# Softmax reciprocals in three bfloat16 parts, and bfloat16 router counts, in an attention and mixture-of-experts kernel

## The chip, the core and the metric

The kernel runs on one core of one Trainium2 chip. The time is the device time of one launch in microseconds (us); lower is better. The core's engines are named as in the profile: PE (TensorE, matrix products), PEld (its weight loads), DVE (VectorE), ACT (ScalarE), POOL (GpSimd) and SP (SyncE, which here only issues DMAs).

## The reference

One transformer layer over x of shape (8, 1024, 256), 16 heads of 16 channels, everything in float32. Cut to what matters here:

```python
scores = einsum('bhid,bhjd->bhij', q, k) * scale + gated_bias   # bias by relative position, gated per query
attn = softmax(scores, axis=-1)
out = einsum('bhij,bhjd->bhid', attn, v)                         # then @ Wo.T + bo
x = layernorm(x + attention(x))

probs = softmax(x_flat @ Wr.T)                                   # router, 8 experts, top 2
for e in range(8):
    elig = (topk_experts == e).any(-1) & ~fallback
    pos = cumsum(elig) - 1                                       # place of each token in expert e
    kept, overflow = elig & (pos < cap), elig & (pos >= cap)     # cap = 2560
    # y of expert e to the kept tokens; the overflow goes to a fallback FFN
x = layernorm(x + moe(x))
```

## The kernel before

The kernel has two stages: attention with the router (until about 2560 us of the profile) and the experts' FFNs (the rest). The change touches the first stage alone.

**Units and steps.** Attention is worked in 64 units: 8 batches times 8 pairs of heads (`HP = 2`). A unit has 16 steps, one for each block of 128 keys (`j`, 8 of them) and each half of the queries (`c`, 512 columns). The loop `for g in range(G + 12)` runs over 1024 steps, `u, s = divmod(g, 16)`. The order of all instructions is written out by hand (`tc.manual_schedule()`), so each engine executes in the order in which the Python code issues.

In a step, `max_fold` (DVE, L1066) first finishes a row maximum; then `streams.held()` reads what a helper task has in its bank; `scores` (PE, L1109) makes two 512-column products; `max_first` and `max_second` (PE, L1025 and L1029) compute exact maxima of the scores 21 steps ahead, in two halves, from bfloat16 parts; `exps` adds the gated bias to the scores (DVE, L1124) and exponentiates (ACT, L1131). On every second step (`c == 1`) `products` (PE, L1139) accumulates probabilities times values in `o_acc`. The values carry a column of ones, so that row `D` of each head's 32 rows of `o_acc` holds the softmax sums. POOL makes the gated biases (`gb`, L985, one for every two steps) and small diagonals (`dgb`, L998).

**Dividing by the sums.** At step 1 of unit `u`, `take_outputs(u - 1)` copies `o_acc` to `osb` (ACT, L1151). The sums lie in 4 rows of 512. Four DMAs move them to 128 partitions x 16, DVE inverts them there (L1172), and four DMAs move them back to 4 rows; `after(n, f)` runs `f` at the n-th following `tick()`, which is in `streams.free()` of each step. So the sums are moved at step 2, inverted at step 4 and moved back at step 5. At step 10 `divide` makes one matmul of `sel` (4 x 128) with the 4 rows (L1179), which spreads the reciprocals over the 16 channels of each head in the one shared PSUM bank (`ps_x`, one buffer); DVE multiplies them onto `osb` (L1183) and four DMAs store the result. All these DMAs are issued by SP, in order, with the loads for unit `u + 2` (`load_unit`, at steps 3, 4 and 6, L907 and L915) and the gates (`load_gates`, L965).

**Helper tasks.** The projections of the next batch (`prologue`), and the output projection, layernorm and router of the batch before (`epilogue`), are Python generators that are advanced once a step, between the steps' own work. A task that needs PSUM takes the shared bank at one step and reads it at the next.

**Counting.** For each expert, POOL makes running counts over the 8 blocks of 128 tokens (`running`, on `prefix` and `incl`, L751), and PE adds them over the partitions (`count`): a product of `ones` with the running counts and one of `later` with `who`, both 128 x 128 by 128 x 8 in float32 (L821, L822). DVE takes the places from it (`place`, `spill`, L835 and L838), and POOL needs `spill` for the next expert. There are 9 such counts for each batch, the last batch's after the loop, where nothing else runs.

**Experts.** Each of 8 experts computes chunks of 512 rows (L1481, L1496), which PE fills.

Of the kernel before, what the change touches and what calls it, by code (L numbers as in the profile page):

```python
# [11 lines left out]
F32 = mybir.dt.float32  # L12
BF16 = mybir.dt.bfloat16
# [3 lines left out]
ALU = mybir.AluOpType  # L17
# [4 lines left out]
P = 128  # L22
H, D = 16, 16
NG, HG = 4, 4
E = H * D
NE, TOP_K = 8, 2
FF = 1024
NBUCKET, MAX_DIST = 80, 200
CH = 512
# [49 lines left out]
def tile_attention_moe(  # L79
# [25 lines left out]
    nc = tc.nc  # L105
    B, N, _ = x.shape
    T = B * N
    NI = N // P
# [44 lines left out]
    with ExitStack() as at:  # L153
        cst = at.enter_context(tc.tile_pool(name="cst", bufs=1))
# [3 lines left out]
        rt = at.enter_context(tc.tile_pool(name="rt", bufs=1))  # L158
# [24 lines left out]
        def load_piece(b, n, tag="xp", bufs=3):  # L183
# [18 lines left out]
            out=gb_ld.rearrange("p g o -> p (g o)"), in_=gru_b.to_broadcast([P, 8])  # L202
# [9 lines left out]
        for sb, src in ((wk_sb, wk), (wq_sb, wq)):  # L212
            for k in range(NK):
                nc.scalar.dma_start(
                    out=sb[:, k, :].rearrange("p (h d) -> p h d", d=D),
                    in_=src[k * P : (k + 1) * P, :].rearrange("p (h w) -> p h w", w=32)[
                        :, :, :D
                    ],
# [3 lines left out]
            out=heads_b[0], in_=kcl[8, :].rearrange("(h w) -> h w", w=32)[:, :D]  # L222
        )
        for g in range(H // HG):
            nc.scalar.dma_start(
                out=heads_b[1, g * HG : (g + 1) * HG, :],
                in_=bq[:, g].rearrange("(r w) -> r w", w=32)[:HG, :D],
            )
        for sb, which in ((bk_sb, 0), (bq_sb, 1)):
            nc.scalar.dma_start(  # L230
                out=sb,
                in_=heads_b[which].rearrange("h d -> (h d)").rearrange("(k p) -> p k", p=P),
# [33 lines left out]
        for base, sign in ((0, 1), (D - 1, -1)):  # L266
            nc.gpsimd.affine_select(
                out=wg, in_=wg, compare_op=ALU.is_ge, fill=0.0, base=base,
                pattern=[[sign * P, NK], [-sign * D, H], [0, 2]], channel_multiplier=sign,
# [6 lines left out]
            out=anti, in_=anti, compare_op=ALU.not_equal, fill=1.0, base=-(P - 1),  # L276
            pattern=[[1, P]], channel_multiplier=1,
        )
        ones = cst.tile([P, P], F32, name="ones")
        nc.gpsimd.memset(ones, 1.0)  # L280
        later = cst.tile([P, P], F32, name="later")
        nc.gpsimd.memset(later, -1.0)
        nc.gpsimd.affine_select(
            out=later, in_=later, compare_op=ALU.is_gt, fill=0.0, base=0,
            pattern=[[-1, P]], channel_multiplier=1,
        )
        sel = cst.tile([4, 4, 32], F32, name="sel")
        nc.gpsimd.memset(sel, 0.0)
        nc.gpsimd.affine_select(
            out=sel, in_=sel, compare_op=ALU.not_equal, fill=1.0, base=0,  # L290
            pattern=[[-1, 4], [0, 32]], channel_multiplier=1,
        )
        rank = cst.tile([P, NE], F32, name="rank")
        nc.gpsimd.iota(
            rank, pattern=[[-1, NE]], base=NE, channel_multiplier=0,
# [4 lines left out]
            number, pattern=[[P, NI]], base=0, channel_multiplier=1,  # L300
# [22 lines left out]
        for lo, hi in zip(cuts[:-1], cuts[1:]):  # L323
# [9 lines left out]
            out=blocks,  # L333
            in_=bass.AP(
                sd.tensor, sd.offset + EDGE + 1 - REACH, [[STRIP, H], [-1, P], [1, WIN]]
            ),
# [15 lines left out]
        for side, bk in enumerate((int(farn[0]), int(far[0]))):  # L352
            nc.sync.dma_start(
                out=farb[:, side, :], in_=rel[bk : bk + 1, :].to_broadcast([P, H])
# [13 lines left out]
        for t in fd:  # L368
# [4 lines left out]
                out=flat, in_=zero16.unsqueeze(1).to_broadcast([P, flat.shape[1], 2 * E])  # L373
# [4 lines left out]
        pattern = once.tile([R_ALL, HP, N], F32, tag="oD", name="pattern")  # L378
        for h in range(HP):
            for part in range(3):  # L380
                r = R_FAR + part * NI
                nc.sync.dma_start(out=pattern[r : r + NI, h, :], in_=kcr[:NI, :])
            for r in range(R_SHIFT, R_ALL):
                nc.sync.dma_start(out=pattern[r : r + 1, h, :], in_=kcr[8:9, :])
        incl = [cst.tile([P, NE + 1, NI], F32, name=f"incl{i}") for i in range(2)]
        prefix = [cst.tile([P, 2 * NI], F32, name=f"prefix{i}") for i in range(3)]
        for t in prefix:
            nc.vector.memset(t, 0.0)
        o_acc = ps_o.tile([P, CH], F32, name="o_acc")
# [54 lines left out]
        def after(n, what):  # L444

            waiting.append([n, what])
# [230 lines left out]
        def epilogue(b, me):  # L677
            xt, oD = me.xt, me.oD
            for t in range(0, NI, 2):
# [3 lines left out]
                for tt in range(2):  # L683
                    for k in range(NK):
# [4 lines left out]
                            start=(k == 0),  # L689
                            stop=(k == NK - 1),  # L690
# [30 lines left out]
            for t in range(0, NI, 2):  # L721
# [13 lines left out]
                for tt in range(2):  # L735
                    for k in range(NK):
                        nc.tensor.matmul(
                            pl[:, tt, :], x1T[:, tt, k, :], wr_sb[:, k, :],
                            start=(k == 0), stop=(k == NK - 1),
# [4 lines left out]
            def small(tag, *shape):  # L744
                return rt.tile([P, *shape], F32, tag=tag, name=f"{tag}{b}")

            def over_e(a):
# [3 lines left out]
                lambda out, a, b, op=op: nc.gpsimd.tensor_tensor(out, a, b, op)  # L751
# [17 lines left out]
            for k in range(TOP_K):  # L769

                m = small(f"top{k}", NI)
                o = small(f"oh{k}", NI, NE)
                first = small(f"first{k}", NI)
# [31 lines left out]
            now, before = incl[b % 2], incl[(b + 1) % 2]  # L805
            live = slice(NI, 2 * NI)
            who = prefix[0][:, live]
# [10 lines left out]

            def count(e):
                pc = bank("pc")[:, :NI]  # L820
                nc.tensor.matmul(pc, ones, now[:, e, :], start=True, stop=False)  # L821
                nc.tensor.matmul(pc, later, who, start=False, stop=True)  # L822
                return pc

            spill = small("spill", NI)
            for e in range(NE):
# [6 lines left out]
                pc = count(e)  # L833
# [13 lines left out]
            sub(fell, ones[:, :NI], stay)  # L847
            yield BANK
            pc = count(NE)
            yield SLOW  # L850
            nc.vector.tensor_scalar(fbrow, pc, float(FB0 - 1), None, ALU.add)
            if b == B - 1:
                yield BANK
                pf = bank("pf")[:, : NE + 1]
                nc.tensor.matmul(pf, ones, now[:, :, NI - 1], start=True, stop=True)
                yield SLOW
                nc.vector.tensor_copy(counts, pf)
            ts = slice(b * NI, (b + 1) * NI)
# [289 lines left out]
        def take_outputs(u):  # L1148
            me = units[u]
            me.osb = work.tile([P, CH], F32, tag="osb", name=f"osb{u}", bufs=1)  # L1150
            nc.scalar.copy(me.osb, o_acc)  # L1151

            def move_sums():
                me.sums = rt.tile([P, 4 * CH // P], F32, tag="sums", name=f"sums{u}")
                for r in range(4):
                    nc.sync.dma_start(
                        out=me.sums[r * 32 : (r + 1) * 32, :],
                        in_=me.osb[r * 32 + D : r * 32 + D + 1, :].rearrange(
                            "o (p n) -> o p n", p=32
                        ),  # L1160
                    )

            def move_back():
                me.recs = rt.tile([4, CH], F32, tag="recs", name=f"recs{u}")
                for r in range(4):
                    nc.sync.dma_start(
                        out=me.recs[r : r + 1, :].rearrange("o (p n) -> o p n", p=32),
                        in_=me.sums[r * 32 : (r + 1) * 32, :],
                    )

            after(1, move_sums)
            after(3, lambda: nc.vector.reciprocal(me.sums, me.sums))  # L1172
            after(4, move_back)

        def divide(u):
            b, hp = divmod(u, UB)
# [139 lines left out]
        for g in range(G + 12):  # L1316
            u, s = divmod(g, STEPS)
# [3 lines left out]
            if g < G:  # L1321
                if sb == 14:
                    assert not streams.of or streams.of[0][0].__name__ == "scatters"
                    if b:
                        streams.start(epilogue(b - 1, batches[b - 1]))
                    streams.start(begin(b))
                if sb == 60:
                    streams.start(rows(b))
                if u + 2 < UNITS:
                    for which, at_ in enumerate((3, 4, 6)):  # L1330
                        if s == at_:
                            load_unit(u + 2, which)
                    if s == 1:
                        load_max_bias(u + 2)
                    if s == 7:
                        clear_max_bias(u + 2)
                if u + 1 < UNITS:
                    if s == 0:
                        load_bias(u + 1)
                    for which, at_ in enumerate((8, 15)):  # L1340
                        if s == at_:
                            load_gates(u + 1, which)
                if m <= G:
                    max_fold(m - 1)
# [18 lines left out]
            others = s + 1 != SHIFT_AT  # L1363
# [10 lines left out]
            if u and s == 1:  # L1374
                take_outputs(u - 1)
            next(clear, None)

        banks += [(ps_m, "pm0"), (ps_m, "pm1")]
        streams.start(epilogue(B - 1, batches[B - 1]))
        streams.drain()  # L1380

# [3 lines left out]
    with ExitStack() as ex:  # L1385
# [11 lines left out]
            place1, pattern=[[P, IPC]], base=1, channel_multiplier=1,  # L1397
# [245 lines left out]
```

## Time and profile before

| | |
|---|---|
| median of 3 runs | 3657.59 us (3646.69 to 3658.37) |
| profiled execution | 3654.03 us, its span 3652.2 us |
| mean granted TensorE clock | 0.963 |
| busy: PE, PEld | 3277.1 us (90%), 1655.8 us (45%) |
| busy: DVE, ACT, POOL | 1935.0 us (53%), 2047.8 us (56%), 2221.9 us (61%) |
| first to last `osb` copy (64 units) | 172.0 to 2471.8 us |
| after the last unit, router of the last batch | about 2490 to 2556 us |

A group line of the profile reads: line, engine, operation, out<-in by the program's names, sizes, count | busy us, mean ns of one | idle time of the engine just before them, and what ended it. A timeline line reads: start us, length us, engine, line, operation; in brackets the idle time before it and what ended that. Busy times of PE include the modelled end of each matmul, so matmuls that follow each other closely show overlapping lengths, and the cost of one is read from the next one's start.

### The profile page before, as it was taken

To read this page: it belongs to the slowest core of one execution; us is meant where nothing else is said; L and a number is where in the kernel's file an instruction comes from. 1 tells how busy PE (TensorE), PEld (TensorE's weight loads), DVE (VectorE), ACT (ScalarE), POOL (GpSimd) and SP (SyncE) were. 2 spreads that over 40 slices of the span, in tenths; PEclk is the share of its full clock that TensorE was granted. 3 is DMA by queue.
4 is the path that set the end of the run, shared out by engine and by line. 5 is a ranking of instruction groups with operands and counts; after the bars stand their busy time and mean duration, and the time that the engine had idled before them with its cause. 6 is when DMAs were issued, how large, how long until landed. Compare 5 with 4: busy or idle time off the path is not lost. (4 is left out here: it accounts for less than half of the span.)

```text
span 3652.2 us, 53430 instructions
## 1 busy us (share of the span) xinstructions
PE 3277.1 (90%) x16263; PEld 1655.8 (45%) x16263; DVE 1935.0 (53%) x5559; ACT 2047.8 (56%) x3084; POOL 2221.9 (61%) x2619
## 2 busy tenths in 40 slices
PE   4798998989999999999999999994399999999997
PEld 2342343334334334334334433333267677667776
DVE  2455656655765665665666576661134344444443
ACT  1577777767777777777787777771022222222222
POOL 2667666876886887787787788782233333333332
PEclk8899999999999999999999999995699999999999
DMA  5567657655643453444444444420332332232220
GB/s 139 159 167 196 190 167 192 186 177 177 186 146 111 139 155 114 130 141 135 125 135 137 133 135 129 132 92 10 113 88 58 88 90 67 85 96 88 72 90 21
DMA packets 380418, 455.71 MB, mean 125 GB/s; under 512 B 87478, under 2 KB 285235, under 8 KB 380107
## 3 DMA queue, kind: packets, MB, share of 16 engines
q1 hardware_dynamic: 338602, 388.06, 35.9%
q0 software_dynamic: 19296, 43.38, 4.2%
q10 hardware_dynamic: 22208, 20.58, 1.9%
q8 instruction: 138, 2.26, 0.3%
q14 instruction: 174, 1.42, 0.1%
HBM read 315.16 MB, written 140.54 MB: 125 GB/s over the span
## 5 line engine op out<-in xcount | busy, mean ns | idle before, releaser
L1131 ACT ACTIVATE pr<-sc 128x1024 f32<-128x1024 f32 x1024 | 1049.0, 1025 | 321.5 <-DVE sc L1124 298.9
L985 POOL TENSOR_TENSOR gb<-bias,gates 128x1024 f32<-128x1024 f32 (+2 forms) x512 | 1070.2, 2091 | 133.6 <-DMA gates<-gd 67.3
L1066 DVE CUSTOM_DVE_ANT_0 over<-pm,over 128x512 f32<-128x512 f32 x1024 | 703.8, 687 | 794.4 <-ACT over L1054 303.9
L1054 ACT ACTIVATE over<-pm 128x512 f32<-128x512 f32 x1024 | 612.7, 598 | 260.9 <-PE pm L1029 242.1
L1109 PE MATMUL sc<-qs,ks 122*128 122x512 bf16 x2048 | 617.4, 382 | 39.2 <-ACT pr L1131 24.7
L1124 DVE TENSOR_TENSOR sc<-sc,gb 128x640 f32<-128x640 f32 (+3 forms) x768 | 599.6, 781 | 77.6 <-POOL gb L985 56.0
L1029 PE MATMUL pm<-biasb,dgb 128*128 128x320 bf16 (+2 forms) x2048 | 579.2, 283 | 0.0
L1139 PE MATMUL o_acc<-pr,v 128*17 128x512 f32 x4096 | 551.9, 610 | 0.3 <-ACT pr L1131 0.3
L1481 PE MATMUL ph<-xsT,w 128*128 128x512 f32 (+1 forms) x1440 | 488.8, 497 | 13.3 <-ACT xsT L1421 12.7
L1496 PE MATMUL py<-w,hT 128*128 128x256 f32 x2208 | 485.0, 379 | 5.5 <-DVE ys L1503 5.5
L1496 PEld LDWEIGHTS py<-w,hT 128*128 128x128 f32 x2208 | 419.2, 190 | 74.1 <-issue 10.5
L1025 PE MATMUL pm<-ks,qs 120*128 120x512 bf16 x1024 | 396.5, 387 | 44.8 <-DVE mh L1066 25.7
L1025 PEld LDWEIGHTS <-qs 120*128 120x128 bf16 x2048 | 207.3, 101 | 505.2 <-issue 339.6
L1025 PE MATMUL pm<-ks_d,qs 120*128 120x512 bf16 x1024 | 393.9, 385 | 39.3 <-DMA qs<-qd 18.0
L1488 ACT ACTIVATE hT<-ph,b_sb 128x512 f32<-128x512 f32 (+1 forms) x360 | 212.3, 590 | 287.9 <-PE ph L1481 264.1
L1481 PEld LDWEIGHTS ph<-xsT,w 128*128 128x128 f32 x1440 | 270.7, 190 | 213.8 <-issue 169.1
L1421 ACT COPY xsT<-pt 128x512 f32<-128x512 f32 (+1 forms) x90 | 39.6, 490 | 567.5 <-PE pt L1418 567.5
L143 POOL TENSOR_TENSOR rs<-rstd,neghalf 128x1 f32<-128x1 f32 x138 | 78.3, 568 | 446.8 <-DVE rstd L141 446.4
L1029 PEld LDWEIGHTS <-dgb 128*128 128x128 bf16 x2048 | 201.7, 98 | 262.5 <-issue 147.2
L998 POOL TENSOR_TENSOR dgb<-anti,grev 128x256 bf16<-128x256 f32 x512 | 313.8, 613 | 4.9
L1109 PEld LDWEIGHTS <-ks 122*128 122x128 bf16 x2048 | 197.5, 99 | 221.4 <-issue 70.4
L419 POOL TENSOR_TENSOR parts<-rest,parts 128x512 bf16<-128x512 f32 (+1 forms) x80 | 92.5, 1157 | 239.7 <-ACT parts L418 193.4
(184 smaller groups left out, 2913.3 us busy)
## 6 DMA issues: line engine op xcount, KB each, us to landing
gates<-gd SPq DMA_DIRECT2D x128, 704.0 KB
biasb<-stripb SPq DMA_DIRECT2D x128, 288.0 KB
bias<-blocks SPq DMA_DIRECT2D x64, 512.0 KB
xd<-zero SPq DMA_DIRECT2D x51, 522.0 KB
ks<-kd SPq DMA_DIRECT2D x384, 64.0 KB
qs<-qd SPq DMA_DIRECT2D x384, 64.0 KB
yd<-zero SPq DMA_DIRECT2D x40, 512.0 KB
w<-in_w_dram ACTq DMA_DIRECT2D x16, 1024.0 KB
```

The source lines that it names most:

```text
L985: nc.gpsimd.tensor_tensor(gb_[:, :, off : off + hi - lo], me.bias[:, :, off : off + hi - lo], gates[:, :, lo - at : hi - at], ALU.mult,)
L998: nc.gpsimd.tensor_tensor(dg, anti.unsqueeze(1).to_broadcast([P, HP, P]), batches[b].grev[:, i, hp * HP : (hp + 1) * HP] .unsqueeze(2) .to ...
L1025: nc.tensor.matmul(pm, QS[u % 3][:R_SHIFT, h, i * P : (i + 1) * P], keys, start=True, stop=False)
L1029: nc.tensor.matmul(pm[:, lo:hi, :], dgb[m - h][:, h, :], me.biasb[:, at : at + (hi - lo) * P].rearrange("p (j n) -> p j n", n=P)[:, :, :HALF],
L1054: nc.scalar.activation(me.over, pm, AF.Relu)
L1066: nc.vector.tensor_tensor_reduce(out=me.over, in0=me.rest, in1=me.over, scale=1.0, scalar=-3.0e38, op0=ALU.add, op1=ALU.max, accum_out=me. ...
L1109: nc.tensor.matmul(me.sc[:, h, :], ks[:, h, j * P : (j + 1) * P], qs[:, h, c * CH : (c + 1) * CH], start=True, stop=True,)
L1124: nc.vector.tensor_tensor(sc[:, :, lo - c * CH : hi - c * CH], sc[:, :, lo - c * CH : hi - c * CH], me.gb[j][:, :, off : off + hi - lo], A ...
L1131: nc.scalar.activation(pr, sc, AF.Exp)
L1139: nc.tensor.matmul(o_acc[r : r + D + 1, :], batches[b].v[:, j, hp * HP + h, :], prs[c][:, h, :], start=(j == 0), stop=(j == NI - 1),)
L1481: nc.tensor.matmul(ph[:, :size], w1_sb[:, k, f * P : (f + 1) * P], xsT[:, k, :size], start=(k == 0), stop=(k == NK - 1),)
L1496: nc.tensor.matmul(py, hT[:, f, t * P : (t + 1) * P], w2_sb[:, f, :], start=(f == 0), stop=(f == NF - 1),)
```

## The change

The reciprocals are made and spread differently, and the counts have other types.

- `sums` is one tile of 128 partitions x 64 for the whole stage, its first 32 partitions filled with 1.0 once. Three DMAs, each of all four rows of sums, write three copies of them to partitions 32 to 127, 64 elements in each partition.
- `first`, at step 4, inverts the whole tile (float32, 128 x 64) and copies it to bfloat16 (`rp`). `others`, at step 5, subtracts the copy from the reciprocals on partitions 64 to 127, copies the rest to bfloat16 there, and subtracts again on partitions 96 to 127. So the three copies become three bfloat16 parts that add up to the reciprocal.
- One DMA, at step 6, moves the 96 partitions back to 12 rows of 512 (`recs`, bfloat16), and the spreading matmul of step 10 has 12 rows and bfloat16 operands; `sel` has its ones in three rows for each head.
- `ones16`, `later16`, `incl` and `prefix` are bfloat16, so the counting matmuls are (the counts stay whole numbers of at most 64 before the sum over partitions).

```diff
-        sel = cst.tile([4, 4, 32], F32, name="sel")
+        sums = cst.tile([P, 4 * CH // 32], F32, name="sums")
+        nc.vector.memset(sums[:32], 1.0)
+        ones16 = cst.tile([P, P], BF16, name="ones16")
+        nc.gpsimd.tensor_copy(ones16, ones)
+        later16 = cst.tile([P, P], BF16, name="later16")
+        nc.gpsimd.tensor_copy(later16, later)
+        sel = cst.tile([12, 4, 32], BF16, name="sel")
...
-        incl = [cst.tile([P, NE + 1, NI], F32, name=f"incl{i}") for i in range(2)]
-        prefix = [cst.tile([P, 2 * NI], F32, name=f"prefix{i}") for i in range(3)]
+        incl = [cst.tile([P, NE + 1, NI], BF16, name=f"incl{i}") for i in range(2)]
+        prefix = [cst.tile([P, 2 * NI], BF16, name=f"prefix{i}") for i in range(3)]
...
-                nc.tensor.matmul(pc, ones, now[:, e, :], start=True, stop=False)
-                nc.tensor.matmul(pc, later, who, start=False, stop=True)
+                nc.tensor.matmul(pc, ones16, now[:, e, :], start=True, stop=False)
+                nc.tensor.matmul(pc, later16, who, start=False, stop=True)
...
             def move_sums():
-                me.sums = rt.tile([P, 4 * CH // P], F32, tag="sums", name=f"sums{u}")
-                for r in range(4):
+                for a in range(3):
                     nc.sync.dma_start(
-                        out=me.sums[r * 32 : (r + 1) * 32, :],
-                        in_=me.osb[r * 32 + D : r * 32 + D + 1, :].rearrange(
-                            "o (p n) -> o p n", p=32
-                        ),
+                        out=sums[(a + 1) * 32 : (a + 2) * 32, :],
+                        in_=me.osb[D::32, :].rearrange("r (p n) -> r p n", p=8),
                     )
+            def first():
+                nc.vector.reciprocal(sums, sums)
+                me.rp = rt.tile([P, 4 * CH // 32], BF16, tag="rp", name=f"rp{u}")
+                nc.vector.tensor_copy(me.rp, sums)
+            def others():
+                nc.vector.tensor_tensor(sums[64:], sums[64:], me.rp[64:], ALU.subtract)
+                nc.vector.tensor_copy(me.rp[64:], sums[64:])
+                nc.vector.tensor_tensor(me.rp[96:], sums[96:], me.rp[96:], ALU.subtract)
             def move_back():
-                me.recs = rt.tile([4, CH], F32, tag="recs", name=f"recs{u}")
-                for r in range(4):
-                    nc.sync.dma_start(
-                        out=me.recs[r : r + 1, :].rearrange("o (p n) -> o p n", p=32),
-                        in_=me.sums[r * 32 : (r + 1) * 32, :],
-                    )
+                me.recs = rt.tile([12, CH], BF16, tag="recs", name=f"recs{u}")
+                nc.sync.dma_start(
+                    out=me.recs.rearrange("q (p n) -> q p n", p=8), in_=me.rp[32:]
+                )
             after(1, move_sums)
-            after(3, lambda: nc.vector.reciprocal(me.sums, me.sums))
-            after(4, move_back)
+            after(3, first)
+            after(4, others)
+            after(5, move_back)
```

In the built program PE, ACT and POOL keep their order otherwise. SP's order changes in one place: the move back stands behind the seven loads of step 6 (`qs<-fd`, `qs<-qd`) and no longer in front of them.

More of the change, by code (lines that the diff above doesn't have):

```diff
@@ L286, in tile_attention_moe @@
         )
-        sel = cst.tile([4, 4, 32], F32, name="sel")
-        nc.gpsimd.memset(sel, 0.0)
-        nc.gpsimd.affine_select(
-            out=sel, in_=sel, compare_op=ALU.not_equal, fill=1.0, base=0,
-            pattern=[[-1, 4], [0, 32]], channel_multiplier=1,
-        )
+        sums = cst.tile([P, 4 * CH // 32], F32, name="sums")
[5 more added lines that the diff above has]
+        sel = cst.tile([12, 4, 32], BF16, name="sel")
+        nc.gpsimd.memset(sel, 0.0)
+        for a in range(3):
+            nc.gpsimd.affine_select(
+                out=sel, in_=sel, compare_op=ALU.not_equal, fill=1.0, base=-4 * a,
+                pattern=[[-1, 4], [0, 32]], channel_multiplier=1,
+            )
         rank = cst.tile([P, NE], F32, name="rank")
@@ L384, in tile_attention_moe @@
                 nc.sync.dma_start(out=pattern[r : r + 1, h, :], in_=kcr[8:9, :])
-        incl = [cst.tile([P, NE + 1, NI], F32, name=f"incl{i}") for i in range(2)]
-        prefix = [cst.tile([P, 2 * NI], F32, name=f"prefix{i}") for i in range(3)]
+        assert B * NI <= 256
+        incl = [cst.tile([P, NE + 1, NI], BF16, name=f"incl{i}") for i in range(2)]
+        prefix = [cst.tile([P, 2 * NI], BF16, name=f"prefix{i}") for i in range(3)]
         for t in prefix:
@@ L854, in epilogue @@
                 pf = bank("pf")[:, : NE + 1]
-                nc.tensor.matmul(pf, ones, now[:, :, NI - 1], start=True, stop=True)
+                nc.tensor.matmul(pf, ones16, now[:, :, NI - 1], start=True, stop=True)
                 yield SLOW
@@ L1153, in move_sums @@
             def move_sums():
-                me.sums = rt.tile([P, 4 * CH // P], F32, tag="sums", name=f"sums{u}")
-                for r in range(4):
+                for a in range(3):
                     nc.sync.dma_start(
-                        out=me.sums[r * 32 : (r + 1) * 32, :],
-                        in_=me.osb[r * 32 + D : r * 32 + D + 1, :].rearrange(
-                            "o (p n) -> o p n", p=32
-                        ),
-                    )
-            def move_back():
-                me.recs = rt.tile([4, CH], F32, tag="recs", name=f"recs{u}")
-                for r in range(4):
-                    nc.sync.dma_start(
-                        out=me.recs[r : r + 1, :].rearrange("o (p n) -> o p n", p=32),
-                        in_=me.sums[r * 32 : (r + 1) * 32, :],
-                    )
+                        out=sums[(a + 1) * 32 : (a + 2) * 32, :],
+                        in_=me.osb[D::32, :].rearrange("r (p n) -> r p n", p=8),
+                    )
+            def first():
[6 more added lines that the diff above has]
+                nc.vector.tensor_tensor(me.rp[96:], sums[96:], me.rp[96:], ALU.subtract)
+            def move_back():
+                me.recs = rt.tile([12, CH], BF16, tag="recs", name=f"recs{u}")
+                nc.sync.dma_start(
+                    out=me.recs.rearrange("q (p n) -> q p n", p=8), in_=me.rp[32:]
+                )
             after(1, move_sums)
-            after(3, lambda: nc.vector.reciprocal(me.sums, me.sums))
-            after(4, move_back)
+            after(3, first)
+            after(4, others)
+            after(5, move_back)
         def divide(u):
```

## The prediction

> **What bounds it.** I read the page's shares and slices first: PE, with the highest share, is busy in nine tenths and more of nearly every slice, and the granted clock is 0.96 to 1.00 in the attention stage once it runs.
>
> ```profile
> PE 3277.1 (90%) x16263; PEld 1655.8 (45%) x16263; DVE 1935.0 (53%) x5559; ACT 2047.8 (56%) x3084; POOL 2221.9 (61%) x2619
> ...
> PE   4798998989999999999999999994399999999997
> ```
>
> Then I cut the stage into its 64 units by the score matmuls. The mean is 36.7 us. Units 8k+5 and 8k+6 take 31 us with PE idle for 0.4 to 0.7. Two steps without helper work take 1.15 + 2.2 = 3.35 us, and the starts of PE's own matmuls account for 3.3: PE sets the pace. In units 8k+7 and 8k POOL also issues 16 scatters (1.01 us each), and the score adds start as POOL's `gb` ends; there POOL sets it, and PE time saved is worth nothing.
>
> By groups (busy, mean ns):
>
> ```profile
> L1179 PE MATMUL pb<-recs,sel 4*128 4x512 f32 x128 | 72.5, 646 | 19.0 <-DMA recs<-sums 9.0 <-DVE dif L651 5.2 <-DVE mh L1066 2.8
> ...
> L1172 DVE RECIPROCAL sums<-sums 128x16 f32<-128x16 f32 x64 | 15.7, 245 | 15.8 <-DMA sums<-osb 15.1 <-issue 0.6
> ```
>
> Every float32 matmul runs as two passes (x128 for 64 units), and so do the counts (L821 and L822, 144 passes each). PE's timeline around one spreading matmul:
>
> ```profile
> 1908.90 1.12 PE L1179 MATMUL pb<-recs,sel 4*128 4x512 f32 x2
> 1909.96 0.39 PE L1025 MATMUL pm<-ks,qs 120*128 120x512 bf16 x1
> 1910.18 0.25 PE L1029 MATMUL pm<-biasb,dgb 128*128 128x192 bf16 x1
> 1910.27 0.59 PE L1109 MATMUL sc<-qs,ks 122*128 122x512 bf16 x2
> 1912.44 0.38 PE L1025 MATMUL pm<-ks_d,qs 120*128 120x512 bf16 x1 [1.57 <-DMA qs<-qd]
> ```
>
> **Spreading matmul.** Start to next start is 1.06 us. A bfloat16 matmul of 512 columns takes 0.22 from start to next start (1909.96 to 1910.18); with part of a weight load (98 ns in L1029's row) I take 0.26. Gain 0.80 in the 48 units that POOL does not pace: 38 us. Bounds: 24 (0.5 each, if DVE's reads in steps 10 to 12, 3.9 us, end last) and 54 (0.85 in all 64).
>
> **Counts.** In the loop a count's four passes hold PE for 0.36 to 0.46 us before the next matmul. Two bfloat16 products with hidden loads should take 0.16 (between 0.06 and 0.2, two loads of L1029's row). That is 0.25 x 63 = 16 us, of which I count 70%, since some fall in steps where PE waits: 11 (bounds 0 and 20). The last batch's nine counts are a bare chain: POOL's `incl` ends at 2530.52, DVE's `place` starts at 2531.63, 1.11 us later. Half the passes save half: 0.55 x 9 + 0.4 for the last sum = 5 (3 to 7). POOL's 128x8 operations take 198 ns, fixed cost at that size; I leave them, and so the five setup operations on POOL, which run beside the first loads (1.5 us if they did not).
>
> **SP's queue.** SP issues `sums` (four, 2.44 us), the loads of steps 3 and 4, and then, without a pause:
>
> ```profile
> 1904.69 2.44 SPq L1166 DMA_DIRECT2D recs<-sums  x4
> 1907.18 0.55 SPq L907 DMA_DIRECT2D qs<-fd  x1
> 1907.77 2.67 SPq L915 DMA_DIRECT2D qs<-qd  x6
> ```
>
> One of four 0.61-us issues goes, and 2.44 us no longer stand in front of `qs<-qd`, so those loads land 3.05 us earlier. PE waits for them at step 11 in 13 units (18 us in all, as in the 1.57 above); all these waits are shorter than 3.05. About half lie in units that POOL paces: gain 9 (0 to 18). The move back itself is now behind the seven loads, so its last issue ends 2.45 us before `qs<-qd` ended, and small DMAs land 1.4 to 1.8 us after that (the sums issued until 947.45 and 1310.40 let the reciprocals start at 948.92 and 1312.20). In those 13 units the matmul then meets it 0 to 0.9 us late; PE executes in order, so every score behind it waits: minus 3 (0 to 10). SP in turn waits for the last subtraction before it moves back, and behind that stand the gates of step 8 and the stores of step 10; the seven loads in front take 3.2 us, longer than `others`, so I count nothing (1 us in each POOL-paced unit if not). The three copies of the sums land 0.6 earlier; the reciprocal's 15.1 us of waiting shrinks a little, not counted.
>
> **VectorE.** A reciprocal of 8 elements (L765) takes 203 ns, of 16 (L1172) 245, so 5.25 ns an element; 64 elements take 0.50 us, 0.25 more. Four more operations follow, some 0.15 each if nothing stops them. But an operation whose inputs both lie in SBUF stands still while POOL works:
>
> ```profile
> 618.10 2.10 POOL L985 TENSOR_TENSOR gb<-bias,gates 128x896 f32<-128x896 f32 x1
> ...
> 618.43 1.85 DVE L776 TENSOR_TENSOR oh<-pp,top 128x64 f32<-128x64 f32 x1
> ...
> 620.14 0.62 POOL L998 TENSOR_TENSOR dgb<-anti,grev 128x256 bf16<-128x256 f32 x1
> ```
>
> It ends 0.08 us after POOL's `gb` (620.20); with POOL quiet it takes 0.22. L776 (16 times) has a mean of 1.24, L781 (the same size) 0.92. Copies of 16x15 take 0.44 in L318, while POOL works, and 0.15 in L325, where it rests, so I let copies wait too. POOL itself is not slowed: the `dgb` above takes its usual 0.61 to 0.62. The new subtractions and copies depend on each other, and POOL's next operation gets in between. I laid the four, in order, over POOL's rows after each of the 63 reciprocals: they and the longer reciprocal add 3.2 us to DVE in a unit, 2.4 of it at step 5. What covers it is DVE's idle time there, for instance 0.86 here:
>
> ```profile
> 1282.02 0.69 DVE L1066 CUSTOM_DVE_ANT_0 over<-pm,over 128x512 f32<-128x512 f32 x1 [0.86 <-ACT over L1054]
> 1282.08 2.37 POOL L985 TENSOR_TENSOR gb<-bias,gates 128x1024 f32<-128x1024 f32 x1
> ...
> 1282.64 0.83 DVE L1124 TENSOR_TENSOR sc<-sc,gb 128x640 f32<-128x640 f32 x1
> ```
>
> If one of them meets that `gb`, the maximum of 1282.02 starts at 1284.5, the add and the exponential behind it are 2.5 late, and with 0.8 us between that exponential's end and the score matmul that reuses its buffer, PE loses 1.7. Over the units 8k+1 to 8k+6 this comes to 0.7 each, 33 us for 48 (in the others POOL makes up for it). Bounds: 5 (copies and subtractions slip between POOL's operations) and 100 (half of 3.2 in 63 units).
>
> The Trainium skill (SBUF — State Buffer, "Who interferes with whom") speaks against this part: a DVE operation with two SBUF inputs contends with a reading GpSimd operation, copies in a two-port mode contend as well, and whoever comes second waits for the whole instruction. Its rule agrees with L776's rows for subtractions; that a copy to bfloat16 of 128x64 does this no row here shows. By the rule all four wait, as I have it; by the narrower reading of the rows only two, which would halve the 33.
>
> **Sum** against the profiled 3654.0 (3652.2 and 1.8 around it; 3.6 under the median): gains 38 + 11 + 5 + 9 = 63, losses 33 + 3 = 36, so 27 less: **3627 us**, on its own 3600 to 3643. A difference under 0.3% (11 us) is what a measurement here cannot tell from none.
>
> **Rivals.** (a) VectorE's stalls end last. For: at step 7 of unit 12 an L781 of 1.81 us lengthens the step to 3.95, against 2.2 without helpers, so nearly all passes to PE. Against: step 5's add is short (0.29), and idle time follows. If half of 3.2 us passes in all units it is 100 + 3 - 63 = +40: 3694, slower. It decides from 1.0 us lost in each of 63 units. (b) The stalls stay in the cover: 5 + 3 - 63 = -55: 3599. For: 1.3 us of cover on average, and small POOL operations with gaps in half the units. (c) It doesn't do what it says for time: PE waits as long as it now works, for the late `recs` (26 us if 40 units wait 0.65) and for ACT (3.25 us in each 3.35): about 3654.
>
> **Chances.** The sum as written 0.45, (a) 0.30, (b) 0.13, (c) 0.12. So faster 0.58, same 0.12, slower 0.30. The range reaches from (b), 3592, to near (a)'s price, 3688.
>
> **What would show it.** One L1179-like matmul per unit near 0.38 us (the row's mean for 512 bfloat16 columns), no more `qs<-qd` waits at step 11, nine shorter counts after 2500 us. The two subtractions and two copies with means of 0.5 to 1 us instead of 0.15 confirm the wait; means under 0.25 refute it and move the time to (b). A PE wait for `recs` over 10 us in all, or DVE's score add waited for by ACT for 60 us more than now, means (c) or (a).

## The result and the profile after

The changed kernel takes 3668.14 us (median of 20 runs), the kernel before 3654.6 in the same comparison: ratio 1.0033 [1.0025, 1.0041], 12 us slower. Forecast were 27 us less. The profiled execution's span went from 3652.2 to 3669.5, 17.3 more: between the first and the last score matmul 28.7 were lost, behind it (the end of the router's chain, then the experts) 10.4 won.

The page after, engine shares and PE's slices, to be held against the first fence of the prediction:

```profile
PE 3231.0 (88%) x16054; PEld 1626.9 (44%) x16054; DVE 2136.2 (58%) x5816; ACT 2033.7 (55%) x3084; POOL 2223.1 (61%) x2623
...
PE   4798998989999999999999998884399999999998
```

PE has 46 us less work and is done later; DVE has 201 us more. DVE's new groups and the matmul (busy, mean ns):

```profile
L1196 PE MATMUL pb<-recs,sel 12*128 12x512 bf16 x64 | 24.4, 382 | 17.9 <-DMA recs<-rp 9.2 <-DVE dif L661 5.2 <-DVE mh L1076 2.3
...
L1172 DVE RECIPROCAL sums<-sums 128x64 f32<-128x64 f32 x64 | 34.8, 544 | 12.7 <-DMA sums<-osb 12.5
...
L1174 DVE CAST rp<-sums 128x64 bf16<-128x64 f32 x64 | 46.5, 727 | 2.2
...
L1177 DVE TENSOR_TENSOR sums<-sums,rp 64x64 f32<-64x64 f32 x64 | 44.9, 702 | 2.0
...
L1178 DVE CAST rp<-sums 64x64 bf16<-64x64 f32 x64 | 71.6, 1119 | 2.2
...
L1179 DVE TENSOR_TENSOR rp<-sums,rp 32x64 bf16<-32x64 f32 x64 | 29.7, 464 | 2.2
```

The four operations take some 0.2 us at their shortest and 3.0 per unit on average, so copies wait for POOL as subtractions do. With the longer reciprocal (0.30) this is 3.3 us per unit; the prediction had 3.2. Who waits for that is in the list of waits (us in total, times, longest):

```profile
ACT pr L1141 <- DVE sc L1134: 402.0, 496, 4.3
...
PE pm L1035 <- DVE mh L1076: 72.1, 118, 2.6
```

In the trace of before the two lines are:

```profile
ACT pr L1131 <- DVE sc L1124: 298.9, 467, 4.6
...
PE pm L1025 <- DVE mh L1066: 25.7, 54, 2.4
```

One of these places as the timeline shows it, steps 5 to 7 of unit 33 (kind 8k+1, that is one of the units 1, 9, 17 and so on):

```profile
1382.75 0.22 DVE L1177 TENSOR_TENSOR sums<-sums,rp 64x64 f32<-64x64 f32 x1
...
1382.80 2.12 POOL L995 TENSOR_TENSOR gb<-bias,gates 128x896 f32<-128x896 f32 x1 [3.48 <-DVE sc L1134]
...
1383.01 1.97 DVE L1178 CAST rp<-sums 64x64 bf16<-64x64 f32 x1
...
1384.89 0.60 POOL L1008 TENSOR_TENSOR dgb<-anti,grev 128x256 bf16<-128x256 f32 x1
...
1385.01 0.57 DVE L1179 TENSOR_TENSOR rp<-sums,rp 32x64 bf16<-32x64 f32 x1
...
1385.61 0.69 DVE L1076 CUSTOM_DVE_ANT_0 over<-pm,over 128x512 f32<-128x512 f32 x1
...
1388.82 0.66 PE L474 MATMUL pt<-ident,xp 128*128 128x128 f32 x4 [2.09 <-DVE mh L1076]
```

The copy waits for `gb`, the next subtraction for `dgb`; the maximum of 1385.61 and all behind it on DVE are late, and PE's transposes for the next batch, which need the shared bank that a maximum reads, wait 2.09 us. What follows no term of the prediction covered. Windows of the same core (length; busy time and instructions of PE, PEld, DVE, ACT, POOL; granted TensorE clock, DMA share, GB/s):

```profile
1372.00:1386.00 14.00, 14.00 (x82) 7.45 (x83) 10.03 (x19) 9.11 (x14) 9.88 (x10) 1.00 0.35 106
...
1388.80:1398.60 9.80, 9.78 (x40) 5.56 (x40) 6.29 (x20) 4.52 (x6) 0.18 (x1) 0.53 0.11 40
```

Behind the wait PE works for 9.8 us at a granted clock of 0.53: a pair of score products takes 1.06 us instead of 0.60.

### The profile page after: what moved, and what is told of

Read it like the earlier page. It is cut to its first block, busy times and chain, and to the rows that moved or that the text cites. A ratio compares the mean times of both kernels' runs of the same rounds, so it can differ in the third digit from the quotient of the medians.

```text
span 3669.5 us, 52666 instructions
## 1 busy us (share of the span) xinstructions
PE 3231.0 (88%) x16054; PEld 1626.9 (44%) x16054; DVE 2136.2 (58%) x5816; ACT 2033.7 (55%) x3084; POOL 2223.1 (61%) x2623
```

## Experiments

Theory 1: VectorE's copies and subtractions wait for POOL, PE then waits for VectorE, and this eats what the matmuls save. Rivals: the mere number of operations or the longer way to `recs`, the moved DMAs, or gains smaller than thought. Ratios are against the kernel before; 0.001 is 3.65 us.

Unit u divides the sums of unit u - 1; in the code below `u` is the unit whose sums they are, and `UB` is 8. To see where time goes I add the units by kind, from the starts of the score matmuls in each trace, as a difference from the trace of before (us). Each row is one profiled execution, and executions of the changed kernel alone lie between 3656 and 3675 us, so entries of a few us tell nothing:

| kernel | 8k | 8k+1 | 8k+2 to 8k+6 | 8k+7 | loop | behind it |
|---|---|---|---|---|---|---|
| changed | 2 | 27 | -14 | 14 | 29 | -10 |
| counts alone | -2 | 3 | -5 | 3 | -2 | -8 |
| stalls alone | 11 | 21 | 18 | 26 | 77 | -1 |
| quiet | 6 | -3 | -39 | -10 | -46 | -11 |
| `others` out in 8k+1 | 5 | -7 | -17 | 12 | -8 | -10 |
| quiet in 8k+7, 8k | 9 | 39 | -21 | -12 | 15 | -10 |
| quiet in 8k+7, 8k, 8k+1 | 8 | -5 | -14 | -13 | -25 | -16 |

### What the stalls cost in all

**The stalls alone, on the kernel before** (`own`, `own16` are constants of 128x64):

```diff
-            after(3, lambda: nc.vector.reciprocal(me.sums, me.sums))
+            def first():
+                nc.vector.reciprocal(me.sums, me.sums)
+                nc.vector.tensor_copy(own16, own)
+            def others():
+                nc.vector.tensor_tensor(own[64:], own[64:], own16[64:], ALU.subtract)
+                nc.vector.tensor_copy(own16[64:], own[64:])
+                nc.vector.tensor_tensor(own16[96:], own[96:], own16[96:], ALU.subtract)
+            after(3, first)
+            after(4, others)
             after(4, move_back)
```

> The kernel before with the four VectorE operations alone, on constants of their own: a copy of 128x64 to bfloat16 behind each reciprocal, and one step later subtraction, copy and subtraction of 64 and 32 partitions. Nobody reads their results and nothing else is moved. Theory 1: the losses of steps 5 to 9 come with them, some 125 us and something back in the POOL-paced units: 80 to 125 more than before, ratio 1.022 to 1.034. Theory 2 (the losses come from the moved DMAs or the longer chain): 0.8 us on VectorE beside 1.3 us of idle time, 0 to 10 more, ratio 1.000 to 1.003.

Measured: 3725.51 us, ratio 1.0192 [1.0171, 1.0212], 70 us slower. Its two copies as groups:

```profile
L1182 DVE CAST own<-own 64x64 bf16<-64x64 f32 x64 | 71.8, 1122 | 2.2
...
L1178 DVE CAST own<-own 128x64 bf16<-128x64 f32 x64 | 51.7, 808 | 0.1
```

Nothing reads what these make, and they cost 70 us: slightly under what theory 1 expected, and far from the 0 to 10 of the rival.

**The change without the stalls** (`me.rp` is bfloat16, `dull` a constant of 128x8).

```diff
-                nc.vector.reciprocal(sums, sums)
-                nc.vector.tensor_copy(me.rp, sums)
+                nc.vector.reciprocal(me.rp[32:64], sums[32:64])
+                nc.vector.reciprocal(dull, dull)
...
-                nc.vector.tensor_tensor(sums[64:], sums[64:], me.rp[64:], ALU.subtract)
-                nc.vector.tensor_copy(me.rp[64:], sums[64:])
-                nc.vector.tensor_tensor(me.rp[96:], sums[96:], me.rp[96:], ALU.subtract)
+                for _ in range(3):
+                    nc.vector.reciprocal(dull, dull)
```

> The changed kernel with as many VectorE operations at the same places, none of which reads two SBUF inputs or copies: the reciprocal writes the bfloat16 part itself, and four reciprocals of 128x8 stand for the copies and subtractions. It leaves out the second and third part of the reciprocals (they are zero). If the waits for POOL are what costs, the stalls that were 70 when put in alone go: 65 to 80 less than the changed kernel, about 3595, ratio to before 0.983. If it is the number of operations or the moved DMAs: as the changed kernel, 1.003. In between (the four operations, 0.8 us on VectorE, still cost 10 to 20): ratio 0.987.

Measured: 3591.73 us, ratio 0.984 [0.982, 0.986]. The same number of operations at the same places, 0.20 us each, and the kernel is 58 us faster than before and 70 faster than the changed one (1.0033 - 0.984 = 0.0193). (An earlier expectation, made before the stalls alone had run, was a ratio of 0.975.) The move back no longer waits for `others` here, but that is not what helps: PE waits 18.2 us for `recs`, against 9.2 in the changed kernel. Put in alone and taken out alone, the stalls cost the same 70: the rival of number and place is out.

### Where they cost it

**`others` left out in units 8k+1** (`if u % UB == 0: return`, with parts two and three preset to zero):

> The changed kernel, with the second and third part of the reciprocals (the step of two subtractions and one copy) left out in the 8 sets of sums that are divided in units 8k+1, and nothing else. If the waits cost the same wherever they fall, this is an eighth of some 125 us: 15 less than the changed kernel, ratio to before 0.999. Theory 1 with the clock: units 8k+1 lose 5 us each, because PE's wait of 2.1 us is followed by some 10 us at half the granted clock: 35 to 40 less, ratio 0.993, and the steps at low clock in these units go from 9 to 0 or 1.

Measured: 3634.04 us, ratio 0.9958 [0.9942, 0.9975]: 27 us less than the changed kernel, from an eighth of the units; in the trace this kind of unit falls by 34. Six of the eight units now take 44.8 us each; four of these took 50.8. The steps at low clock in them fell from 9 to 3, not to 0 or 1, and the time that the clock's record is low in them from 55 us to 7, as it was before the change.

**PE's wait filled with work.** Is it the idle time that halves the clock?

```diff
                 yield BANK
+                if b and n == NI // 2 - 1:
+                    fill = ps_m.tile([P, CH], F32, tag="pm0", name="fill")
+                    for _ in range(8):
+                        nc.tensor.matmul(fill, ones16, junk, start=True, stop=True)
                 pt = bank("pt")
```

> The changed kernel with eight matmuls added that nobody needs (bfloat16, 512 columns, 1.7 us together at full clock), put on PE in units 8k+1 just ahead of the transposes that wait there for VectorE; the wait itself stays. If PE's idle time brings the half clock, the granted clock stays at 1.0 behind it and seven units win 3 to 3.5 us each less what the added matmuls overhang (up to 0.5): 15 to 25 less than the changed kernel, ratio to before 0.997 to 0.999. If the clock falls for another reason (the float32 transposes, the work of the other engines), the steps stay at 0.53 and the time is the same or up to 5 longer: 1.003 to 1.005.

The same unit, PE's timeline and the windows behind it:

```profile
1385.20 1.90 PE L475 MATMUL fill<-junk,ones 128*128 128x512 bf16 x8
1387.35 0.66 PE L480 MATMUL pt<-ident,xp 128*128 128x128 f32 x4 [0.25 <-DVE mh L1082]
```

```profile
1385.00:1387.10 2.10, 2.10 (x12) 0.70 (x8) 2.03 (x6) 1.42 (x2) 0.00 (x0) 1.00 0.43 137
1387.10:1396.90 9.80, 9.07 (x54) 4.98 (x54) 7.35 (x25) 6.25 (x10) 2.08 (x3) 1.00 0.12 47
```

The transposes still wait for the same maximum, but the clock stays at 1.00, and this unit takes 46.45 us instead of 50.75. Without the stall it took 44.77. So of the 6.0 us that such a unit loses, 1.7 are the wait and 4.3 the half clock. In the changed kernel PE waits 2.1 us at this place in six units; behind five of them the clock halves, and the sixth, unit 25, where it doesn't, takes 46.45 as well. The kernel as a whole won only 5 us (ratio 1.0019 [1.0008, 1.0029]; the interval overlaps that of the changed kernel, so 5 is rough), less than expected. In the trace units 9, 17, 33 and 49 each won 2.9 to 4.4, but in unit 41 the first copy now waited 6.08 us behind POOL, and that unit grew by 2.8.

Why unit 25 kept its clock can be read from the record of the granted clock, which in this trace changes only at points of a regular grid, 3.41 us apart. In each of the five places the whole wait lies between two such points (in unit 33 the wait is 1386.72 to 1388.82, the points are 1385.96 and 1389.37), and the clock is low from the second one on. In unit 25 a point of the grid, 1092.41, falls inside the wait of 1091.49 to 1093.59 and leaves 0.92 us on one side and 1.17 on the other. This fits all six places; no run moved a wait to test it.

**`others` left out in 8k+7 and 8k** (`if u % UB in (6, 7): return`), the kinds where the prediction held that POOL makes up for the stalls:

> The changed kernel, with the second and third part of the reciprocals (two subtractions and a copy) left out in units 8k+7 and 8k alone, where POOL also issues the scatters. The prediction held that POOL makes up for stalls there: then the time stays, ratio to before 1.003. The stalls put in alone lengthened these two kinds of unit by 25.5 and 11.4 us: then 30 to 40 less than the changed kernel, ratio 0.993 to 0.996.

Measured: 3662.05 us, ratio 1.0035 [1.0022, 1.0049]: nothing gained. **And in 8k+7, 8k and 8k+1:**

> The changed kernel, with the second and third part of the reciprocals left out in units 8k+7, 8k and 8k+1 together. Left out in 8k+1 alone the ratio to before was 0.9958, in 8k+7 and 8k alone 1.0035 (nothing gained, and steps 3 to 5 behind them longer by what steps 7 to 9 won). If POOL's own backlog of scatters carries 8k+7 and 8k whatever VectorE does, as the prediction had it, this kernel is as the one with 8k+1 alone: 0.994 to 0.996. If their stalls count and were only hidden by those of 8k+1, some 15 us more come off: 0.990 to 0.993.

Measured: 3652.51 us, ratio 1.0004 [0.9993, 1.0016], slower than with 8k+1 alone, which neither expectation allowed. The timeline shows why, step 4 of unit 25:

```profile
1078.19 6.10 DVE L1177 CAST rpz<-sums 64x64 bf16<-64x64 f32 x1
1078.20 0.61 POOL L1010 TENSOR_TENSOR dgb<-anti,grev 128x256 bf16<-128x256 f32 x1
...
1078.78 2.34 POOL L997 TENSOR_TENSOR gb<-bias,gates 128x1024 f32<-128x1024 f32 x1
...
1081.09 0.61 POOL L1010 TENSOR_TENSOR dgb<-anti,grev 128x256 bf16<-128x256 f32 x1
1081.66 2.33 POOL L997 TENSOR_TENSOR gb<-bias,gates 128x1024 f32<-128x1024 f32 x1
...
1083.96 0.68 DVE L1078 CUSTOM_DVE_ANT_0 over<-pm,over 128x512 f32<-128x512 f32 x1
```

The one copy that I had left in waits through four POOL operations that follow each other without a gap. In six of the eight units 8k+1 it took 5.8 to 6.8 us here, and 0.20 in all eight in the changed kernel: with 8k+7 and 8k shorter, POOL reaches 8k+1 with a backlog and meets the copy. So these two runs mixed two things, and two more took the copies away as well.

**Neither copy nor subtraction in 8k+7, 8k and 8k+1** (bfloat16 reciprocal written directly, parts two and three zero):

> The changed kernel, with the reciprocal written to bfloat16 directly and neither copy nor subtraction (second and third part left out) in units 8k+7, 8k and 8k+1. In the run that left out the step of three alone, the one copy that stayed in 8k+1 waited 6 us behind POOL in most of them, so that run could not tell. If stalls in 8k+7 and 8k count once those of 8k+1 are gone too: the three kinds of unit come to what they take in the quiet kernel, 50 us less than in the changed kernel: ratio to before 0.989 to 0.991. If POOL's backlog carries 8k+7 and 8k whatever VectorE does: as with the step left out in 8k+1 alone, 0.994 to 0.996.

Measured: 3615.05 us, ratio 0.9906 [0.9889, 0.9923]. **In 8k+7 and 8k alone:**

> The same in units 8k+7 and 8k alone; 8k+1 keeps its copies and subtractions. If POOL makes up for the stalls of 8k+7 and 8k, as the prediction held, nothing is gained: ratio to before 1.001 to 1.004, and the copy behind the reciprocal in 8k+1 waits some 6 us again, because the earlier start of these units leaves POOL without a gap there. If the stalls count: 20 to 30 less than the changed kernel, 0.995 to 0.998, with that copy at 0.2.

Measured: 3656.45 us, ratio 1.0014 [1.0004, 1.0024], 7 us less than the changed kernel, with the copy in 8k+1 at 6 us again in six units. So the stalls of 8k+7 and 8k do count, but in full only once those of 8k+1 are gone: 0.9958 - 0.9906, 19 us. While 8k+1 keeps its copy, what is won in 8k+7 (26 us in the table) comes back in 8k and 8k+1 (19 us).

### What the parts of the change gain

**The counts alone** (`ones16`, `later16`, `incl`, `prefix` in bfloat16 on the kernel before):

> The kernel before with the counts alone as bfloat16 matmuls (ones16, later16, incl, prefix); the reciprocals stay as they were. My prediction's terms for this were 11 us in the loop and 5 us for the last batch's chain, so 16 less than before: ratio 0.9956. The traces of before and after show the stretch behind the last score matmul 10.4 us shorter, which contains the chain. If counts hidden in steps where PE waits anyway are the rule, only the chain is left: 5 to 10 less, ratio 0.998. If the setup operations on POOL cost something that is not covered: 1.000 or above.

Measured: 3638.22 us, ratio 0.9962 [0.9949, 0.9975]: 14 us, as expected; by itself this part is faster than both kernels. In its trace 8 lie behind the last score matmul and 2 in the loop, but that execution (3645.95) is the longest of six; by the median the loop may have won some 6.

**The order alone** (`after(4, move_back)` becomes `after(5, move_back)` on the kernel before, four DMAs):

> The kernel before with the four move-back DMAs issued one step later, behind the seven loads of step 6, and nothing else. My prediction's terms: the loads of qs land 2.44 us earlier (not 3.05, all four DMAs of the sums stay), 13 waits of PE at step 11 (18 us in the trace of before) go, half of them where POOL paces: 9 less, and 3 back for a late recs: 6 less, ratio 0.998. If all 18 us count: ratio 0.995. If the four issues of the move back, now 2.44 us long behind the loads, arrive later than the spreading matmul in most units (about 1 us in 30 units): ratio 1.007.

Measured: 3690.83 us, ratio 1.0112 [1.0092, 1.0131], 41 us slower, near the last of the three cases and beyond it. Its waits:

```profile
PE pb L1179 <- DMA recs<-sums: 76.8, 30, 8.9
```

**The order undone in the changed kernel** (`after(4, move_back)`, one DMA):

> The changed kernel with the one DMA of the move back issued at step 5, ahead of the seven loads of step 6, as the kernel before has its four; nothing else. The prediction gave the order 9 less the 3 of a late recs: then 6 us more than the changed kernel, ratio to before 1.005, and PE's waits for qs at step 11 are back in part (one issue of 0.61 instead of four). Rival: SP now waits in front of the loads for the last subtraction, which ends up to 4 us late, and the loads land later than before: 15 to 25 more, ratio 1.008 to 1.010. Other rival: with one DMA instead of four the loads are early enough and recs 3 us earlier: 3 to 8 less, ratio 1.001 to 1.002.

Measured: 3672.99 us, ratio 1.0061 [1.0041, 1.0080], 10 more than the changed kernel, between the first expectation and the first rival; the two intervals touch, so 10 is rough. Its trace does not show where the 10 should come from: PE waits for `qs<-qd` at no step 11, as in the changed kernel, it waits 7.5 us for `recs` instead of 9.2, and the two profiled spans are the same (3669.5 us). So the waits for `qs`, 18.0 us in the trace of before, go with one DMA in either order. With four the new order removes them too, but PE then waits 76.8 us for `recs` instead of 9.0.

### The same parts elsewhere

**Copies on ScalarE, subtractions on POOL** (`nc.scalar.copy` and `nc.gpsimd.tensor_tensor` in place of `nc.vector`, one step later):

> The changed kernel with the two copies on ScalarE and the two subtractions on POOL, one step apart (reciprocal at step 4, copy and subtraction at 5, copy and subtraction at 6, move back at 7); the same three parts come out. Theory 1: VectorE has only the reciprocal left of it (0.54), the waits go; ScalarE gets two copies of about 0.2 and POOL two subtractions of about 0.2, which cost 0.5 us in each of 16 POOL-paced units, and recs come one step later (PE waits up to 1 us in some units): 60 to 100 under the changed kernel, 3570 to 3610, ratio 0.977 to 0.988. Theory 2 (the longer chain to recs costs): as slow as the changed kernel or slower, ratio 1.003 to 1.01.

Measured: 3710.9 us, ratio 1.0166 [1.0147, 1.0186]. Each operation now waits for another engine's, in queues that run in order: POOL waits 65.2 us for the second copy and 44.8 for the first, ACT 29.0 for the subtraction between them. Theory 1 alone was too simple here.

**All four on POOL, at step 5** (`nc.gpsimd` in place of `nc.vector`):

> The changed kernel with both copies and both subtractions on POOL, one behind the other, at step 5; VectorE keeps the reciprocal, and the same three parts come out. POOL's operations stand in its own queue, so nothing of them waits for another engine's instruction. Theory 1: VectorE's stalls go (70), POOL gets some 1 us per unit, which costs 1 us in the 16 units where it is busy longest, and recs come up to 2 us later where POOL is behind: 35 to 55 less than the changed kernel, 3610 to 3630, ratio to before 0.989 to 0.994. Rival: POOL paces more units than those 16, or recs come too late, as with the copies on ScalarE: ratio 1.003 to 1.015.

Measured: 3644.09 us, ratio 0.9977 [0.9964, 0.999]. That is 20 us less than the changed kernel and better than both, but less than expected: of the 70 us of stalls the larger part is lost again. The trace shows POOL with 1.08 us more per unit and PE waiting 31.1 us for `recs` in place of 9.2; which of the two weighs more was not separated.

**VectorE makes the reciprocal twice, POOL the rest:**

```diff
-                nc.vector.reciprocal(sums, sums)
-                nc.vector.tensor_copy(me.rp, sums)
+                nc.vector.reciprocal(me.rp, sums)
+                nc.vector.reciprocal(sums, sums)
...
-                nc.vector.tensor_tensor(sums[64:], sums[64:], me.rp[64:], ALU.subtract)
-                nc.vector.tensor_copy(me.rp[64:], sums[64:])
-                nc.vector.tensor_tensor(me.rp[96:], sums[96:], me.rp[96:], ALU.subtract)
+                nc.gpsimd.tensor_tensor(sums[64:], sums[64:], me.rp[64:], ALU.subtract)
+                nc.gpsimd.tensor_copy(me.rp[64:], sums[64:])
+                nc.gpsimd.tensor_tensor(me.rp[96:], sums[96:], me.rp[96:], ALU.subtract)
```

> The changed kernel with all three parts: VectorE makes the reciprocal twice (bfloat16 and float32), POOL the subtraction, the copy and the subtraction (0.30 + 0.24 + 0.30). Against all four on POOL (0.998) POOL has a quarter less to do: 0.993 to 0.997. Rival: the second reciprocal (0.54 more on VectorE at step 4) costs more than the copy saved on POOL: 0.999 to 1.003.

Measured: 3634.34 us, ratio 0.9952 [0.9936, 0.9968]. **The same with two parts,** one subtraction on POOL, 8 rows in the matmul:

> The changed kernel with two bfloat16 parts in place of three: VectorE makes the reciprocal twice, once into bfloat16 and once into float32 (0.54 each, neither waits for POOL), POOL makes the one subtraction (0.30), and the matmul has 8 rows. The third part is left out. If the waits of VectorE for POOL are the whole loss, it comes near the quiet kernel (0.984): 0.984 to 0.989. Rival: whatever stands in POOL's queue makes recs late, as with all four operations on POOL (0.998): 0.993 to 0.998.

Measured: 3608.17 us, ratio 0.9887 [0.9867, 0.9906], the fastest version that keeps more than one part; the quiet kernel remains 17 us ahead.

## Why the prediction was wrong

**The sum of the gains was right.** The prediction had 38 + 11 + 5 + 9 less 3 for late `recs`, 60 us without stalls; the quiet kernel is 58 us under the kernel before. Inside that sum the counts were 16 in the prediction and 14 alone. The matmul and the order together were 38 + 9 - 3 = 44, and 58 - 14 = 44 is left for them, but the 38 was not run by itself, and that the 9 comes from the order is not shown: PE's waits for `qs` are gone with the order undone as well. The prediction's reason for counting little for late `recs` holds for one DMA only, as the run with four shows.

**The size of the stalls on DVE was right,** 3.2 us per unit against 3.3, and so was the choice to let copies wait, though one of its two grounds was thin (the 0.44 us of L318 is the mean of 0.72 and 0.16). The Trainium skill (SBUF — State Buffer, "Who interferes with whom") says that a copy in a two-port mode contends with GpSimd and the second blocks for the whole instruction. The runs agree on the copies (0.20 us free, 1.97 behind a `gb` of 2.12), and show that the wait need not end with that instruction: 6.10 us through four of them. So the rule, which the prediction introduced as speaking against this part, spoke for it.

**The step that failed is what passes to PE:** "0.7 each, 33 us for 48 (in the others POOL makes up for it)". By ratios, in the order in which the runs take the stalls away:

| units | predicted | measured |
|---|---|---|
| 8k+2 to 8k+6 (40) | 28 | 24 (0.9906 - 0.984) |
| 8k+1 (8) | 5 | 27 (1.0033 - 0.9958) |
| 8k+7 and 8k (16) | 0 | 19 (0.9958 - 0.9906) |
| all | 33 | 70 |

The 0.7 of the plain units held (24 / 40 = 0.6). In 8k+1 the loss was put with the plain units; there PE waits for a bank that DVE frees, and the half clock that follows costs more (4.3) than the wait (1.7). Over all units the clock's record is low for 133 us in the changed kernel, 74 before and 66 in the quiet kernel, and 48 of the 67 us between the first and the last lie in 8k+1. In 8k+7 and 8k the claim was half true: POOL gives most of the time back as long as something in 8k+1 waits for it, and no longer. The clock has little part in these 19 us: in the two kinds its record is low for 37.5 us with `others` out in 8k+1, and still for 33.5 with all three kinds quiet. The differences between ratios carry some 7 to 10 us of uncertainty each; that 8k+1 costs several times the 5 us predicted does not hang on that.

**The nearest rival** is (a), stalls that end last: its point of decision was 1.0 us for each of 63 units, and 70 / 63 = 1.1. Its price (half of 3.2 everywhere, 3694) was too high by 26 us, and that it came this near is partly luck: it had the same loss in every unit, where the plain units lost 0.6 and those of 8k+1 3.4, and the clock was not in it. Nor does it say much that 3668 lies in the prediction's widest range, 3592 to 3688, which holds nearly all the rivals. Rival (a)'s signs were named rightly: ACT waits for the score add 103 us longer (60 were asked), and PE's waits for `recs` stayed under 10 us.

Still open is through which of PE's waits the plain units, and those of 8k+7 and 8k, lose their time: their losses are known as sums alone.

## What to carry to other kernels

Price an operation that can wait for another engine by the unit in which it waits, not by a mean: a step that is freed, or filled, moves the next collision. Where PE has an order that waits for a late bank, add the clock behind the wait to the wait. And try each part of a change alone: here the counts gain 14 us by themselves, while the reciprocals' gain is lost to four small operations on an engine that waits for another.

## What the runs showed of the hardware

TensorE's granted clock fell (0.53 over the 9.8 us behind unit 33's wait) after a wait of 2.1 us in five of six like places, and stayed at 1.00 where eight unused matmuls filled that wait. The Trainium skill (TensorE: Matmul & The Clock Gate, "Part 1: The HAM clock gate") gives an idle window of about 3.4 us for this; here less was enough. The record changes only at points 3.41 us apart, and in the changed kernel's loop every fall came at the end of such a stretch in which PE had idled for 1.44 us or more; after stretches with up to 1.65 us it could also stay. In the trace of before it fell after seven stretches with 0.7 to 1.0 us as well, so idle time is not the whole rule.

A VectorE copy to bfloat16 can wait through several GpSimd operations that follow without a gap (5.8 to 6.8 us in six of the eight units 8k+1), while a reciprocal of 64 elements, with one input, took 541 to 554 ns in all 64 units of the changed kernel, and writing it to bfloat16 directly cost the same (542).
